# Five groups of instructions kept in the source's order: statistics, square roots, sums on transposes and the inverse's additions

## The chip, the core and the metric

One Trainium2 core runs the whole program. It has five engines, each with a queue of its own that is worked off in order: TensorE for matrix products (PE in the profile; the loads of its stationary operand have a row of their own, PEld), VectorE (DVE), ScalarE (ACT), GpSimd (POOL) and SyncE (SP). DMA transfers are issued from the queues of SP and ACT. The engines meet through semaphores only: an instruction whose operand isn't there yet holds up everything behind it on its own engine. The metric is the device time of one execution in microseconds, as the median of several runs.

## What is computed

`x` holds 32 images of 32 channels of 128 x 128 float32. Two layers with a residual follow each other. The first normalizes pairs of channels and takes a matrix square root of every channel by a Newton-Schulz iteration; the second normalizes again, goes to the frequency domain, mixes channels there for 2 x 32 x 32 modes, and comes back:

```python
    def _L0_conv_ref(A):
        ...
        normA = jnp.sqrt(jnp.sum(A2 * A2, axis=(1, 2)))
        Y = A2 / normA[:, None, None]
        ...
        for _ in range(NUM_ITER):
            T = 0.5 * (3.0 * I - jnp.matmul(Z, Y))
            Y = jnp.matmul(Y, T)
            Z = jnp.matmul(T, Z)
        sA = Y * jnp.sqrt(normA)[:, None, None]
    def _L1_conv_ref(x, weights1, weights2):
        ...
        x_dht = jnp.fft.fftn(x.astype(jnp.complex64), axes=(2, 3)).real
        top = jnp.einsum('bixy,ioxy->boxy', x_dht[:, :, :M1, :M2], weights1)
        bot = jnp.einsum('bixy,ioxy->boxy', x_dht[:, :, -M1:, :M2], weights2)
        ...
        y = jnp.fft.ifftn(out_dht.astype(jnp.complex64), axes=(2, 3)).real
    x = x + _L0_conv_ref(_gn(x))
    x = x + _L1_conv_ref(_gn(x), L1_conv_weights1, L1_conv_weights2)
```

## The kernel before

**The work.** The unit is a group of four channels of one image: 256 groups, eight for each image. A group goes through the generator `newton` in about ten steps. Nine such generators ("lanes") are under way at once; the main loop at the end of the kernel goes round the lanes, and in each round a lane makes one step. Between the lanes the same loop advances the other work: `prep` (first normalization: statistics of two images ahead of their use), `staged` (normalized operands of the next groups), `settle` (what follows when a group is done), `forward` and `spectrum` (towards the frequency domain), the products of the modes, and `inverse` (the way back and the sum that goes to the output). All this is Python that runs when the program is built; the order in which it calls the instructions is what "program order" or "the source's order" means here.

**Who sets the order on an engine.** The instructions go through a scheduler that gives each engine its queue. It may take an instruction earlier than the source has it where, by its own model of time, the operands are there sooner. `kept(...)` (which is `tc.keep_in_program_order`) pins an instruction behind everything that the source has called before on that engine; what comes after it in the source may still be moved ahead of it. So a pinned instruction can only lose the places that the scheduler had let it gain, and those that it had overtaken get them back. Before, the transfers, the operands made in `staged` and the products in `forward` are pinned; most arithmetic isn't.

**What stands around the change.**

- `prep` (L186 on): 16 loads of a tile `xs` for two images, three of them ahead, on the ACT queue (L199), a pool of four buffers; two `bn_stats` on DVE for each (L207) into `a_st`; then the means (L168), two small products on PE (L171, L215), and two calls of `root` (L151), each a Sqrt on ACT (L154) and four or five small DVE instructions, whose results are the scales and offsets `a_sc`, `a_off`, `a_t_s`.
- `staged` (L334 on): four instructions for `x` and four for `b` of a group, on POOL (L349) and ACT (L342), and `plus_eye`, one 128 x 512 addition on POOL into `r` (L295 or L302). A second `plus_eye` for each group stands in `newton`.
- `quartic` (L365 on): for the "far" groups, those of images 1 to 18, a matrix is transposed by way of memory: DVE transposes 32 x 32 blocks into `turn` (L374), SP writes the tile to memory (L376) and reads it back as `w` in another order (L384, L387), POOL adds `r` to it (L389), and one round later PE multiplies by it (through `products`, L308). For all others PE transposes (L314) and DVE adds (L283). Each group has two such places.
- `settle` (L434 on): a finished group's `xt` is stored, and POOL makes `fold` from it in two instructions (L441).
- `summed` (L487 on): the second normalization of an image, with a Sqrt on ACT (L508).
- `inverse` (L841 on): for each half image four PSUM banks `py` are filled (L888). ACT copies two of them into `d` (L900) while DVE adds the other two to `y` (L905), and one round later the roles are swapped. Then POOL adds `d` (L838) and the result is stored. All products share eight PSUM banks.

The far groups end near 1600 us of the profiled execution; `inverse` begins near 1866 us, when the products of the first 20 images are done.

Of the kernel before, what the change touches and what calls it, by code (L numbers as in the profile page):

```python
# [30 lines left out]
AF = mybir.ActivationFunctionType  # L31
ALU = mybir.AluOpType
# [36 lines left out]
def conv_preact_kernel(  # L69
# [81 lines left out]
    def root(v, n, tag):  # L151

        s0 = small.tile([P, n], F32, tag="root_0", name=f"{tag}_s0")
        nc.scalar.activation(s0, v, AF.Sqrt)  # L154
        yield
        q = small.tile([P, n], F32, tag="root_1", name=f"{tag}_q")
        nc.vector.reciprocal(q, s0)
        nc.vector.tensor_mul(q, q, v)
        nc.vector.tensor_tensor(q, q, s0, ALU.add)
        s = small.tile([P, n], F32, tag=f"{tag}_s", name=f"{tag}_s", bufs=2)  # L160
        nc.vector.tensor_scalar_mul(s, q, 0.5)
        return s
# [23 lines left out]
    def prep(bs, made):  # L186

        n = len(bs)
        nc_, ng = n * C, n * G
        first_b = bs[0]  # L190
        st = small.tile([P, ng, 6], F32, tag="a_st", name=f"a_st{first_b}", bufs=2)
        tiles = []
        parts = [(b, i) for b in bs for i in range(C // 4)]

        def load(k):
            b, i = parts[k]
            t = stp.tile([P, 2, 2 * P], F32, tag="xs", name=f"xs{b}_{i}")
            src = xs_in[b, :, 2 * i : 2 * i + 2].rearrange("p g h c -> p g (h c)")
            kept(nc.scalar.dma_start(out=t, in_=src))  # L199
            tiles.append(t)  # L200

        for k in range(3):
            load(k)
        yield
        for k in range(len(parts)):
            for j in range(2):
                nc.vector.bn_stats(st[:, 2 * k + j, :], tiles[k][:, j, :])  # L207
            yield
            if k + 3 < len(parts):
                load(k + 3)  # L210
        ms = small.tile([P, ng], F32, tag="a_ms", name=f"a_ms{first_b}")
        nm, d = yield from moments(st, ms, "a")
        yield from pause
        pq = bank()[:, 0, 0:nc_]
        nc.tensor.matmul(pq, avg_mean, d.rearrange("p g c -> p (g c)"), start=True, stop=True)  # L215

        v = small.tile([P, nc_ + ng], F32, tag="a_v", name=f"a_v{first_b}")
        nc.vector.tensor_scalar_mul(v[:, 0:nc_], pq, -512 / (P * P))
        yield
        vg = small.tile([P, ng], F32, tag="a_vg", name=f"a_vg{first_b}")  # L220
        nc.vector.tensor_reduce(
            vg, v[:, 0:nc_].rearrange("p (g c) -> p g c", c=2), AX.X, ALU.add
        )
        nc.vector.tensor_scalar(v[:, nc_:], vg, 0.5, EPS, ALU.mult, ALU.add)
        yield
        s = yield from root(v, nc_ + ng, "a_r")
        iv = small.tile([P, nc_ + ng], F32, tag="a_inv", name=f"a_inv{first_b}")
        nc.vector.reciprocal(iv, s)
        yield

        sc = small.tile([P, nc_], F32, tag="a_sc", name=f"a_sc{first_b}", bufs=2)
        nc.vector.tensor_scalar_mul(sc, iv[:, 0:nc_], MS / P)
        nn = small.tile([P, ng, 2], F32, tag="a_d", name=f"a_n{first_b}")
        nc.vector.tensor_tensor(  # L234
            nn,
            s[:, 0:nc_].rearrange("p (g c) -> p g c", c=2),
            iv[:, nc_:, None].to_broadcast([P, ng, 2]),
            ALU.mult,
        )
        nn = nn.rearrange("p g c -> p (g c)")  # L240
        nc.vector.tensor_scalar_mul(nn, nn, P * (1.5 / (EYE * QF)) ** 2)
        yield
        sn = yield from root(nn, nc_, "a_t")

        off = small.tile([P, ng, 2], F32, tag="a_off", name=f"a_off{first_b}", bufs=2)
        nc.vector.tensor_tensor(
            off,
            sc.rearrange("p (g c) -> p g c", c=2),
            nm[:, :, None].to_broadcast([P, ng, 2]),
            ALU.mult,  # L250
        )
        off = off.rearrange("p g c -> p (g c)")
        for k, b in enumerate(bs):
            g, c = slice(k * G, k * G + G), slice(k * C, k * C + C)
            made[b] = (nm[:, g], sc[:, c], off[:, c], sn[:, c])
        yield
# [108 lines left out]
    def quartic(m, mb, r, far, more, wide):  # L365


        v = plus(m, -QA * MS, products(mb, m), "v", more)
        if far:


            t = four("turn", more)
            form = "p c (b i) -> p b c i" if wide else "p c (i b) -> p b c i"
            nc.vector.transpose(blocks(t), v.rearrange(form, b=4))  # L374
            held = dram.tile([P, 512], F32, name="turn", tag="turn", bufs=8)
            kept(nc.sync.dma_start(out=held, in_=t.rearrange("p c x -> p (c x)")))  # L376
            yield from rest
            w = four("w", more)
            wb = blocks(w).rearrange("p a c j -> p a (c j)")
            if wide:  # L380
                for b in range(4):
                    rows = slice(32 * b, 32 * b + 32)
                    src = held[:, P * b : P * b + P].rearrange("(a i) x -> i a x", a=4)
                    kept(nc.sync.dma_start(out=wb[rows], in_=src))  # L384
            else:
                src = held.rearrange("(a i) (b x) -> (i b) a x", a=4, b=4)
                kept(nc.sync.dma_start(out=wb, in_=src))  # L387
            yield from rest
            nc.gpsimd.tensor_tensor(w, w, r, ALU.add)  # L389
            w = blocks(w).rearrange("p a c j -> p c a j")  # L390
        else:
            yield from rest
            w = plus(transposed(v), 1.0, r, "w", more)
        yield from rest
        q = plus(products(v, w), QF / (16 * MS**4), eye, "q", more)
        yield from rest
        return q
# [89 lines left out]
    def summed(b, st):  # L487

        mq = small.tile([P, 2, G], F32, tag="b_mq", name=f"b_mq{b}")
        _, d = yield from moments(st, mq[:, 0, :], "b")  # L490
        yield

        nc.vector.tensor_reduce(mq[:, 1, :], d, AX.X, ALU.add)
        wide = small.tile([P, 2, G, 2], F32, tag="b_wide", name=f"b_wide{b}")
        nc.vector.tensor_copy(wide, mq[:, :, :, None].to_broadcast([P, 2, G, 2]))
        wide = wide.rearrange("p k g c -> p k (g c)")
        yield from pause
        pv = bank()[:, 0, :]
        for i in range(4):
            rows = slice(C * i, C * i + C)  # L500
            nc.tensor.matmul(pv[rows, 0:1], wide[:, 1, :], avg_v, start=True, stop=True)
        nc.tensor.matmul(pv[0:C, 1:2], wide[:, 0, :], avg_0, start=True, stop=True)
        v = small.tile([P, 2], F32, tag="b_v", name=f"b_v{b}")
        nc.vector.tensor_scalar(v[:, 0:1], pv[:, 0:1], 1.0, EPS, ALU.mult, ALU.add)
        nc.vector.tensor_copy(v[0:C, 1:2], pv[0:C, 1:2])
        yield
        s = small.tile([P, 3], F32, tag="b_r", name=f"b_r{b}")
        nc.scalar.activation(s[:, 0:1], v[:, 0:1], AF.Sqrt)  # L508
        yield
        nc.vector.reciprocal(s[:, 1:2], s[:, 0:1])  # L510
        nc.vector.tensor_scalar(
            s[:, 2:3], v[:, 0:1], s[:, 1:2], s[:, 1:2], ALU.mult, ALU.mult
        )
        nc.vector.tensor_scalar(s[:, 2:3], s[:, 2:3], -0.5, 1.5, ALU.mult, ALU.add)
        r = small.tile([P, 1], F32, tag="b_inv", name=f"b_inv{b}")
        nc.vector.tensor_mul(r, s[:, 1:2], s[:, 2:3])
        scales[b] = v, r
        yield
# [322 lines left out]
    def inverse(b):  # L841
# [37 lines left out]
        for e in range(2):  # L879
# [16 lines left out]
            for i in range(2):  # L896

                for j in range(2):
                    n = 2 * (1 - i) + j
                    nc.scalar.copy(d[:, 4 * n : 4 * n + 4, :], py[n][:, :, 64:128])  # L900
                for j in range(2):
                    y = yts[b, e][i][:, 4 * j : 4 * j + 4, :]
                    y = y.rearrange("p c (s h) -> p c s h", s=2)
                    half = py[2 * i + j][:, :, None, 0:64].to_broadcast([P, 4, 2, 64])
                    nc.vector.tensor_tensor(y, half, y, ALU.add)  # L905
                unfold()
                sums.append((b, 16 * e + 8 * i, yts[b, e][i], d[:, 8 * i : 8 * i + 8, :]))
                if not i:
                    holding.append(b)
                    yield  # L910
                    holding.pop()
# [201 lines left out]
```

## Time and profile before

| | |
|---|---|
| median of 3 runs | 3047.77 us (3047.1 to 3060.3) |
| profiled execution: its own time / span | 3058.61 us / 3056.7 us |
| mean granted TensorE clock | 0.978 |
| busy: PE / DVE / POOL / ACT | 2901.3 / 2238.3 / 1999.1 / 1638.1 us |
| 512 `bn_stats` on DVE (L207) | 195.8 us, 412 ns each |
| 288 additions on `w` on POOL (L389) | 366.6 us, 1276 ns each |
| 34 + 32 Sqrt on ACT (L154, L508) | about 0.24 us each |
| DMA, mean | 208 GB/s |

The table is read from top to bottom: PE has the most work, and the other engines have a fifth to a half of the span free. A time that an engine waits costs the kernel something only if PE, which follows its own fixed queue, then finds an operand missing or a PSUM bank still in use.

### The profile page before, as it was taken

Reading aid. Unit: us, or ns where it says so; the run is one execution under the profiler, and the core shown is the slowest. Engines: PE = TensorE matmul, PEld = TensorE weight load, DVE = VectorE, ACT = ScalarE, POOL = GpSimd, SP = SyncE. Lnnn points to the kernel's source line nnn. Section 1 sums busy time; section 2 is a strip of 40 time slices with the busy share of each in tenths; the row PEclk is TensorE's granted clock in tenths of the full one; section 3 lists DMA queues with packets and bytes.
Section 4 is the critical chain, followed back from the end, with each engine's and each line's share of the span. In section 5 each row is a group of like instructions: output and inputs, shape, how many; then the busy total and the mean of one; then the engine's idle time right before and its main releaser. Section 6 shows DMA issues by size and latency. Waiting matters only on the chain.

```text
span 3056.7 us, 73392 instructions
## 1 busy us (share of the span) xinstructions
PE 2901.3 (95%) x27076; PEld 2697.1 (88%) x27076; DVE 2238.3 (73%) x4255; ACT 1638.1 (54%) x4187; POOL 1999.1 (65%) x2312
## 2 busy tenths in 40 slices
PE   6999999999999999999999999999899998999994
PEld 6899999999999999999999888898898887888883
DVE  6778787878787878777866545777777765867664
ACT  3566566566565566565545544454454444555552
POOL 4577777776767777777755435676676763777452
PEclk9999999999999999999999999999999998999996
DMA  5476766767576768676733666677667667665675
GB/s 168 159 229 209 218 210 219 222 204 226 187 231 194 242 193 247 186 245 189 232 101 115 190 199 223 204 247 241 205 216 247 219 232 231 205 205 199 194 242 202
DMA packets 476659, 636.40 MB, mean 208 GB/s; under 512 B 97040, under 2 KB 257296, under 8 KB 476304
## 3 DMA queue, kind: packets, MB, share of 16 engines
q1 hardware_dynamic: 362976, 424.31, 43.3%
q10 hardware_dynamic: 113328, 207.41, 21.7%
q8 instruction: 217, 3.56, 0.5%
q14 instruction: 138, 1.13, 0.1%
HBM read 402.42 MB, written 229.11 MB: 207 GB/s over the span
## 4 chain that ended last, share of the span: by engine, by line
PE 76%; DMA 11%; DVE 5%; POOL 3%; ACT 2%; issue 2%; SPq 1%; ACTq 0%; DVEq 0%; POOLq 0%
PE ps L308 50%; PE ps L418 12%; PE ps L314 6%; DMA xs<-in_xs 4%; PE ps L464 2%; DMA w<-turn 1%; PE ps L888 1%; DMA or<-od 1%; PE ps L617 1%; POOL yt L838 1%; PE ps L870 1%; PE ps L529 1%; DVE yt L905 1%; DMA plain<-in_wk 1%; DVE a_st L207 1%
## 5 line engine op out<-in xcount | busy, mean ns | idle before, releaser
L308 PE MATMUL ps<-w,v 128*128 128x128 f32 x4096 | 555.8, 279 | 16.3 <-POOL w L389 6.6
L389 POOL TENSOR_TENSOR w<-w,r 128x512 f32<-128x512 f32 x288 | 366.6, 1276 | 306.5 <-DMA w<-turn 249.5
L342 ACT ACTIVATE b<-b,a_off,a_sc 128x128 f32<-128x128 f32 x1024 | 467.3, 490 | 160.4 <-issue 48.0
L308 PEld LDWEIGHTS ps<-w,v 128*128 128x128 f32 x4096 | 507.6, 194 | 29.2 <-POOL w L389 8.3
L418 PE MATMUL ps<-my,q 128*128 128x256 f32 x2048 | 491.6, 383 | 9.6 <-ACT d L900 6.0
L441 POOL TENSOR_TENSOR fold<-xt 128x256 f32<-128x256 f32 x512 | 364.6, 734 | 170.2 <-DVE xt L428 155.9
L283 DVE SCALAR_TENSOR_TENSOR q<-ps,eye 128x512 f32<-128x512 f32 x512 | 348.2, 680 | 164.4 <-PE ps L308 158.3
L838 POOL TENSOR_TENSOR yt<-yt,d 128x512 f32<-128x512 f32 x248 | 310.5, 1282 | 197.2 <-ACT d L900 150.6
L418 PEld LDWEIGHTS ps<-my,q 128*128 128x128 f32 x2048 | 370.5, 191 | 56.6 <-ACT d L900 6.8
L349 POOL TENSOR_SCALAR x<-xt,a_nm,a_sc 128x128 f32<-128x128 f32 x736 | 324.1, 455 | 18.6 <-DVE a_n L234 18.6
L302 POOL TENSOR_TENSOR r<-mb,eye 128x512 f32<-128x512 f32 x112 | 142.8, 1275 | 295.5 <-ACT mb L275 282.3
L421 ACT ACTIVATE t<-ps 128x256 f32<-128x256 f32 x512 | 192.8, 383 | 231.4 <-PE ps L418 226.5
L424 ACT ACTIVATE y<-ps,a_t_s 128x128 f32<-128x128 f32 x1024 | 312.0, 370 | 0.0
L207 DVE BATCH_NORM_STATS2 a_st<-xs 128x6 f32<-128x256 f32 x512 | 195.8, 412 | 139.1 <-DMA xs<-in_xs 138.6
L308 PE MATMUL ps<-y,t 128*128 128x128 f32 x2048 | 276.5, 279 | 10.4 <-DVE t L283 9.6
L308 PE MATMUL ps<-x,q 128*128 128x128 f32 x2048 | 278.2, 279 | 6.2 <-DVE q L283 6.2
L308 PE MATMUL ps<-x,b 128*128 128x128 f32 x2048 | 277.9, 279 | 5.9 <-POOL x L349 5.7
L407 ACT ACTIVATE my<-ps 128x512 f32<-128x512 f32 x256 | 152.9, 597 | 243.0 <-PE ps L308 238.0
L308 PE MATMUL ps<-my,mb 128*128 128x128 f32 x2048 | 277.3, 279 | 3.1 <-ACT d L900 3.1
L308 PE MATMUL ps<-my,q 128*128 128x128 f32 x2048 | 277.7, 279 | 2.1 <-ACT my L407 2.1
L308 PE MATMUL ps<-q,t 128*128 128x128 f32 x2048 | 275.2, 278 | 1.2 <-ACT d L900 1.2
L308 PEld LDWEIGHTS ps<-my,q 128*128 128x128 f32 x2048 | 262.4, 194 | 14.6 <-issue 2.7
(138 smaller groups left out, 5572.4 us busy)
## 6 DMA issues: line engine op xcount, KB each, us to landing
turn<-turn SPq DMA_DIRECT2D x288, 256.0 KB
b<-in_x ACTq DMA_DIRECT2D x256, 256.0 KB
xt<-in_xt ACTq DMA_DIRECT2D x256, 256.0 KB
xs<-in_xs ACTq DMA_DIRECT2D x256, 256.0 KB
mid<-xt SPq DMA_DIRECT2D x256, 256.0 KB
yt<-mid SPq DMA_DIRECT2D x128, 512.0 KB
out<-yt SPq DMA_DIRECT2D x117, 512.0 KB
w<-turn SPq DMA_DIRECT2D x144, 256.0 KB
```

Source lines behind the costliest of these rows:

```text
L207: nc.vector.bn_stats(st[:, 2 * k + j, :], tiles[k][:, j, :])
L283: nc.vector.scalar_tensor_tensor(s, ps, f, t, ALU.mult, ALU.add)
L308: nc.tensor.matmul(ps[:, j, :], lhsT[:, j], rhs[:, j], start=True, stop=True)
L314: nc.tensor.transpose(ps[:, j, :], t[:, j, :], ident)
L342: nc.scalar.activation(t, x, AF.Identity, bias=offset[:, c], scale=scale[:, c])
L349: nc.gpsimd.tensor_scalar(m[:, j, :], xt[:, j, :], nm[:, c // 2 : c // 2 + 1], sc[:, c : c + 1], ALU.add, ALU.mult,)
L389: nc.gpsimd.tensor_tensor(w, w, r, ALU.add)
L418: nc.tensor.matmul(both[j // 2][:, j % 2], q[:, j], my[:, j], start=True, stop=True)
L421: nc.scalar.mul(w[:, 2 * h : 2 * h + 2, :], both[h][:, :, 1, :], 1 / (MS * QF))
L424: nc.scalar.mul(y[:, j, :], both[j // 2][:, j % 2, 0, :], sn[:, c : c + 1])
L441: nc.gpsimd.tensor_tensor(f[:, :, 64 * half : 64 * half + 64], xt[:, :, 0:64], xt[:, :, 64:128], op)
L838: engine.tensor_tensor(yh, yh, d, op)
```

## The change

`kept` is put around five calls, and nothing else is touched. No instruction is added or removed, and no operand changes.

```diff
     def root(v, n, tag):
...
-        nc.scalar.activation(s0, v, AF.Sqrt)
+        kept(nc.scalar.activation(s0, v, AF.Sqrt))
...
             for j in range(2):
-                nc.vector.bn_stats(st[:, 2 * k + j, :], tiles[k][:, j, :])
+                kept(nc.vector.bn_stats(st[:, 2 * k + j, :], tiles[k][:, j, :]))
...
             yield from rest
-            nc.gpsimd.tensor_tensor(w, w, r, ALU.add)
+            kept(nc.gpsimd.tensor_tensor(w, w, r, ALU.add))
             w = blocks(w).rearrange("p a c j -> p c a j")
...
         s = small.tile([P, 3], F32, tag="b_r", name=f"b_r{b}")
-        nc.scalar.activation(s[:, 0:1], v[:, 0:1], AF.Sqrt)
+        kept(nc.scalar.activation(s[:, 0:1], v[:, 0:1], AF.Sqrt))
...
                     half = py[2 * i + j][:, :, None, 0:64].to_broadcast([P, 4, 2, 64])
-                    nc.vector.tensor_tensor(y, half, y, ALU.add)
+                    kept(nc.vector.tensor_tensor(y, half, y, ALU.add))
```

When both kernels are built and their queues are compared place by place, PE and SP have exactly the same order in both. On the other three engines:

| engine | pinned | what the pin moves | what moves ahead in its stead |
|---|---|---|---|
| DVE | `bn_stats` L207 | 394 of 512 later, up to 20 places | 566 of 1248 of L283 (`v`, `w`, `q`, `t`), 98 of 256 `xt` (L428), 95 of 288 `turn` (L374), up to 14 places |
| DVE | `yt` L905 | 63 of 256 later, up to 7 places | 86 of 256 stand earlier, up to 13 places, since statistics and root arithmetic left their way |
| ACT | Sqrt L154, L508 | 29 of 34 and 5 of 32 later, up to 29 places | copies of the Newton steps, by at most 5 places |
| POOL | `w` L389 | 139 of 288 later, up to 6 places | 141 of 288 `r` (L295), 126 of 736 `x` (L349), 78 of 512 `fold` (L441), by at most 2 places |

All 139 additions on `w` that move lie in the first 1600 us of the profile of before.

## The prediction

> **What bounds the kernel now.** I read the page's first two parts, then PE by stretches.
>
> ```profile
> span 3056.7 us, 73392 instructions
> PE 2901.3 (95%) x27076; PEld 2697.1 (88%) x27076; DVE 2238.3 (73%) x4255; ACT 1638.1 (54%) x4187; POOL 1999.1 (65%) x2312
> ...
> 76.00:1600.00 1524.00, 1513.06 (x12627) 1434.54 (x12626) 1215.33 (x2313) 905.20 (x2349) 1085.09 (x1209) 1.00 0.67 208
> 1866.00:2980.00 1114.00, 1047.20 (x10751) 952.94 (x10751) 788.57 (x1447) 559.12 (x1422) 738.70 (x866) 0.97 0.68 221
> ```
>
> The stretches' columns are bounds, length, busy time of PE, PEld, DVE, ACT, POOL, then granted clock, DMA share, GB/s. PE is the bound, but in two ways. From 76 to 1600 us it is idle for 10.9 us of 1524, at clock 1.00: nothing to win there, much to lose. From 1866 to 2980 it is idle for 66.8 us and the clock averages 0.97: something can be won there. PE's own queue doesn't change, so the question is only which operand or bank is late for it.
>
> The waits name the places:
>
> ```profile
> ACT d L900 <- DVE yt L905: 160.4, 61, 6.3
> DVE a_st L207 <- DMA xs<-in_xs: 138.6, 83, 6.5
> POOL w L389 <- DMA w<-turn: 249.5, 114, 5.8
> ```
>
> DVE waits 138.6 us for statistics whose data haven't landed: they were put too early. ACT waits 160.4 us for `yt`. The timeline shows both in one event of the late stretch:
>
> ```profile
> 2131.62 0.43 DVE L207 BATCH_NORM_STATS2 a_st<-xs 128x6 f32<-128x256 f32 x1 [4.07 <-DMA xs<-in_xs]
> 2131.97 1.27 DVE L905 TENSOR_TENSOR yt<-ps,yt 128x512 f32<-128x512 f32 x2
> 2132.67 0.92 ACT L900 COPY d<-ps 128x256 f32<-128x256 f32 x3 [6.24 <-DVE yt L905]
> 2133.10 1.67 PE L308 MATMUL ps<-w,v 128*128 128x128 f32 x8 [2.42 <-ACT d L900]
> ```
>
> One `bn_stats` waits 4.07 us for its load; `yt` is queued behind it; ACT's copy of the same bank waits 6.24 us for `yt`; PE waits 2.42 us for the bank.
>
> **The change, part by part.**
>
> *Statistics, roots and `yt` on DVE and ACT: a gain, late.* In the changed queue that `bn_stats` stands 20 places later, behind the `yt` pair; the runs of four statistics or of root arithmetic ahead of other `yt` pairs are gone as well. From PE's waits of 1866 to 2980 I add those released by ACT `d` (6.9 + 6.0 + 0.4), DVE `q` (4.7 + 1.8), `w` 2.8, `t` (2.7 + 1.0), `v` 1.7, `a_t_q` 0.9, ACT `my` 4.2 and `z` 3.9: 37 us. Left out are 29 us of other waits (weights and products from memory, `ob`, `b_wide`, `fold`, `gt`), which the change doesn't reach.
>
> Such a wait has a second price. After the one shown, PE's granted clock is 0.57 from 2133.1 to 2136.5; it comes back after 3.4 us, in which half the work is done, so some 1.7 us more. Going through the timeline, ten such slow intervals (eight of some 3.4 us with two of 6.8, 41 us together) follow the waits that I counted; at half speed that is 20 us. A full gain would be 57 us. Against it: 63 of the 256 `yt` additions go later by up to 7 places, 0.68 us each (L283's row); these are mostly a half image's second pair, which now stands a round later and keeps two of the eight PSUM banks in the meantime. If a quarter of the 63 met a PE waiting for the bank, by one place each, 11 us would go back, and other waits of that size remain. I take 40 us; bounds 10 and 57.
>
> *Cover for what is pinned later.* The roots' results have time: `a_off` is written at 906.9 and first read at 950.1 us, the others 34 to 90 us ahead, against at most 25 places on DVE or 29 on ACT, under 20 us. The means `a_ms` move by at most 12 places, 9 us, and PE takes them 18 us or more after their end where they move most, 5.5 us or more elsewhere, where they move by at most 7 (3.8 us). Cost nothing; without that cover PE would wait at L171, 17 times, a few us each. Later statistics also free their `xs` buffer later, and the load that wants it stands in ACT's queue, with all copies of the Newton steps behind it. The load comes two steps of `prep` after the statistics of its buffer, 7 us or more; nothing again, and 12.1 us is what ACT loses to this release now (its wait on `a_st` at L342).
>
> *The sum on POOL: a loss, early.* `w` is different: PE takes it one round after it is called, and it is now queued behind `r`, `x` and `fold` of other groups. `fold` waits for `xt`, which DVE has only just been asked for. An instance:
>
> ```profile
> 1173.46 1.28 POOL L295 TENSOR_TENSOR r<-mb,eye 128x512 f32<-128x512 f32 x1
> 1174.69 1.30 POOL L389 TENSOR_TENSOR w<-w,r 128x512 f32<-128x512 f32 x1
> 1175.84 0.64 DVE L428 TENSOR_TENSOR xt<-ps,xt 128x512 f32<-128x512 f32 x1
> 1178.19 1.45 POOL L441 TENSOR_TENSOR fold<-xt 128x256 f32<-128x256 f32 x2
> 1178.26 1.06 PE L308 MATMUL ps<-w,v 128*128 128x128 f32 x8
> 1179.61 0.89 POOL L349 TENSOR_SCALAR x<-xt,a_nm,a_sc 128x128 f32<-128x128 f32 x2
> 1180.45 1.28 POOL L295 TENSOR_TENSOR r<-b,eye 128x512 f32<-128x512 f32 x1
> ```
>
> The `w` of 1174.69 ends at 1175.99; PE multiplies by it at 1178.26, a margin of 2.3 us. In the changed queue two `fold`, two `x` and one `r` come first. `fold` can't start before `xt` ends at 1176.5 (DVE's order gives `xt` no earlier place here): 1176.5 + 1.45 + 0.89 + 1.28 + 1.30 = 1181.4, so PE waits 3.2 us.
>
> I did this sum for all 139 that move: start of each instruction now ahead no sooner than its operand in this trace, `w` no sooner than its transfer landed, 1.276 us for it, and `xt` put earlier where statistics leave its way on DVE. 107 are still in time (the median margin of a moved `w` was 4.2 us). 32 come late, by 57 us together; 70 us if `xt` gains nothing. 11 of them exceed 2.1 us; every wait of PE over that in this trace is followed by a slow interval, most by 3.4 us. The 4.2 us wait at 139.9, which has this very pattern already (`r`, two `x`, `w`), is followed by clock 0.53 from 144.0 to 150.8 with PE busy for 4.86 of 6.8 us, so a slow 3.4 us costs 1.7 x 4.86 / 6.8 = 1.2 us: 11 x 1.2 = 13. I take 57 + 13 = 70 us. Upper bound: 70 plus 20 waits of 1.6 us or more at the full 1.7, 34: 104. Lower bound from what stands in this order already: of 11 `w` that directly follow two `fold`, two `x` and one `r` in this trace, two kept PE waiting (4.2 and 1.9 us); 48 of the moved get a `fold` ahead, 48 x 2 / 11 x 3.0 us = 26.
>
> [...]
>
> `r`, `x`, `v`, `q` and `turn` that come earlier in this stretch win at most PE's 10.9 us of idle time, of which `w` itself causes 6.6; I take nothing.
>
> *Start and end.* The first 46 us of DVE's queue are the same as before, and of PE's last 77 us the waits hang on one image's chain: nothing.
>
> **Sum.** 70 - 40 = +30 us on 3058.6 us, 1.0%. The profiled execution lies 10.8 us above the median of the runs; set on the median: 3047.8 + 30 = 3078. Under 0.5%, 15 us, I call it no change, about what the spread of the three runs (13 us) lets one tell.
>
> **Rivals.**
>
> *The sums keep their margin, and the late gain stays.* POOL is 71% busy in the early stretch, so it could catch up, and a PE that waited once gives the next `w` its wait as margin. For it: 9 of 11 in the same order are in time. Against it: the moved ones are those that a late `fold` separates from their place, and most of the late ones lie 20 to 60 us apart, too far to share a wait. Price: 26 + 5 of clock - 57 = -26: 3022.
>
> *The two cancel.* Loss near 55, gain near 50: within 15 us of 3048.
>
> *The second `yt` pair takes the banks.* This ends well above: the half image's banks 3 and 4 are held a round longer, PE waits for them at the next allocation, and the late gain shrinks to 10. It decides once the release falls behind the eighth following use of a bank, 7 to 8 us of PE work at 0.9 us a bank. For it: PE's largest waits there are for just these banks. Against it: most such pairs move by one or two places only. 3048 + 70 - 10 = 3108.
>
> That the change doesn't do what it says is excluded by the queues as built.
>
> **Numbers.** Forecast (3063 to 3100) 0.45; sums keep their margin 0.27; cancel 0.13; banks 0.15. Slower 0.45 + 0.15 = 0.60, same 0.13, faster 0.27. Range: all at its worst is 3048 + 104 - 10 = 3142 and at its best 3048 + 26 - 57 = 3017; the worst needs every bound at once, so I cut it to 3120, and give the best 5 us for waits of ACT that I counted as nothing: 3012.
>
> **What would show it.** Right: PE's wait on POOL `w` L389 grows from 6.6 to 40 us or more before 1600, with a granted clock below 1.00 there and POOL `fold` directly ahead of late `w`; DVE's wait on `xs` falls from 138.6 to under 30, ACT's on `yt` from 160.4 to about half, PE's on ACT `d` from 13 to under 4; 1866 to 2980's stretch is shorter by some 40 us. Wrong: the stretch to 1600 us keeps its length (then the first rival), or new waits of PE on `yt` L905 appear (the last one).

## The result and the profile after

The changed kernel takes 3072.32 us (median of 7 runs, 3064.6 to 3082.47), the kernel before in the same sitting 3048.67 us (7 runs, 3047.1 to 3060.3). The ratio is 1.0082, with an interval of 1.0061 to 1.0103: slower by 24 us. The profiled execution took 3078.48 us, 6 us above the median of its kernel; that of before lay 10 us above its own.

The first two parts of the changed kernel's page, and PE by stretches (columns as before). PE's queue is the same in both kernels, so the bounds are set where the same PE instructions stand; 77.30 to 1672.69 answers to 76 to 1600 of before, and 1937.25 to 2999.34 to 1866 to 2980:

```profile
span 3076.5 us, 73387 instructions
PE 2900.9 (94%) x27076; PEld 2696.2 (88%) x27076; DVE 2244.6 (73%) x4255; ACT 1640.8 (53%) x4187; POOL 1996.1 (65%) x2312
...
77.30:1672.69 1595.39, 1533.29 (x12628) 1448.83 (x12626) 1219.20 (x2316) 908.44 (x2349) 1083.43 (x1209) 0.99 0.64 198
1672.69:1937.25 264.56, 261.30 (x2913) 239.82 (x2912) 152.75 (x303) 128.80 (x310) 123.61 (x170) 1.00 0.56 172
1937.25:2999.34 1062.09, 1022.86 (x10751) 933.92 (x10750) 789.26 (x1445) 558.55 (x1423) 736.44 (x865) 0.99 0.71 232
```

The same work takes 71.4 us longer early on (1595.4 against 1524.0) and 51.9 us less late (1062.1 against 1114.0); the piece between the two stretches, the start and the end make up +0.3. That is the whole difference of the spans, 19.8 us. Length minus PE's busy time is its idle time: early it goes from 10.9 to 62.1 us, late from 66.8 to 39.2. The rest is busy time of the same PE instructions: 20.2 us more early (granted clock 1.00 to 0.99) and 24.3 us less late (0.97 to 0.99).

The waits of the whole run (who waits, on whom: sum in us, how many, the longest):

```profile
ACT d L900 <- DVE yt L905: 137.2, 59, 7.1
POOL w L389 <- DMA w<-turn: 78.6, 49, 3.8
PE ps L308 <- POOL w L389: 59.8, 31, 3.2
DVE a_st L207 <- DMA xs<-in_xs: 25.3, 16, 6.4
```

DVE hardly waits for `xs` any more (138.6 before), and POOL waits less for transposes from memory (249.5), since its `w` now comes later. But PE waits for that `w` 31 times, 59.8 us; before it was three times, 6.6 us.

The loss can be read in the very place for which the prediction worked out a wait of 3.2 us, in the changed kernel's timeline (start, duration, engine, line and operation; in brackets the idle time before it and who ended it):

```profile
1231.38 1.44 POOL L441 TENSOR_TENSOR fold<-xt 128x256 f32<-128x256 f32 x2 [1.81 <-DVE xt L428]
1232.81 0.87 POOL L349 TENSOR_SCALAR x<-xt,a_nm,a_sc 128x128 f32<-128x128 f32 x2
1233.65 1.25 POOL L295 TENSOR_TENSOR r<-b,eye 128x512 f32<-128x512 f32 x1
1234.87 2.48 POOL L389 TENSOR_TENSOR w<-w,r 128x512 f32<-128x512 f32 x2
1236.18 1.87 PE L308 MATMUL ps<-w,v 128*128 128x128 f32 x8 [3.19 <-POOL w L389]
```

`fold` waits 1.81 us for `xt`, then `fold`, `x` and `r` run, and only then `w`: PE stands for 3.19 us. In two stretches of 3.4 us of the same trace, before and after that moment, the clock is the third number from the end:

```profile
1233.00:1236.40 3.40, 0.22 (x2) 0.22 (x3) 1.67 (x4) 1.14 (x3) 3.40 (x5) 1.00 0.89 311
1236.00:1239.40 3.40, 3.22 (x16) 3.22 (x17) 1.31 (x4) 0.72 (x2) 2.58 (x3) 0.56 0.86 274
```

PE works through the 3.4 us after its wait at a granted clock of 0.56. The gain can be read where before one `bn_stats` waited 4.07 us for its load (at 2131.62 there); the same event in the changed kernel:

```profile
2176.96 1.15 PE L888 MATMUL ps<-gt,tab 32*128 32x260 f32 x16
2177.51 0.67 DVE L283 SCALAR_TENSOR_TENSOR q<-ps,eye 128x512 f32<-128x512 f32 x1
2178.12 1.29 DVE L905 TENSOR_TENSOR yt<-ps,yt 128x512 f32<-128x512 f32 x2
2178.85 0.92 ACT L900 COPY d<-ps 128x256 f32<-128x256 f32 x3 [2.21 <-DVE yt L905]
2180.72 1.06 PE L308 MATMUL ps<-w,v 128*128 128x128 f32 x8
```

No statistics stand ahead of `yt`; ACT's copy waits 2.21 us instead of 6.24, and PE (last line) finds its bank free and doesn't wait, where it waited 2.42.

### The profile page after: what moved, and what is told of

Its sections match the earlier page's. It is cut to its first block, busy times and chain, and to the rows that moved or that the text cites. A ratio compares the mean times of both kernels' runs of the same rounds, so it can differ in the third digit from the quotient of the medians.

```text
span 3076.5 us, 73387 instructions
## 1 busy us (share of the span) xinstructions
PE 2900.9 (94%) x27076; PEld 2696.2 (88%) x27076; DVE 2244.6 (73%) x4255; ACT 1640.8 (53%) x4187; POOL 1996.1 (65%) x2312
## 4 chain that ended last, share of the span: by engine, by line
PE 57%; DMA 6%; DVE 5%; POOL 4%; issue 2%; ACT 1%; SPq 1%; ACTq 0%; POOLq 0%; DVEq 0%
PE ps L308 36%; PE ps L418 9%; PE ps L314 5%; PE ps L888 2%; PE ps L464 1%; PE ps L617 1%; PE ps L870 1%; DVE yt L905 1%; POOL w L389 1%; DMA w<-turn 1%; POOL r L295 1%; POOL fold L441 1%; PE ps L529 1%; PE ps L687 1%; DMA yt<-mid 1%
## 5 line engine op out<-in xcount | busy, mean ns | idle before, releaser
L308 PE MATMUL ps<-w,v 128*128 128x128 f32 x4096 | 557.6, 280 | 68.7 <-POOL w L389 59.8
L308 PEld LDWEIGHTS ps<-w,v 128*128 128x128 f32 x4096 | 506.6, 194 | 85.8 <-POOL w L389 67.3
L441 POOL TENSOR_TENSOR fold<-xt 128x256 f32<-128x256 f32 x512 | 364.0, 732 | 253.6 <-DVE xt L428 196.5
L283 DVE SCALAR_TENSOR_TENSOR q<-ps,eye 128x512 f32<-128x512 f32 x512 | 349.7, 683 | 234.4 <-PE ps L308 229.1
L389 POOL TENSOR_TENSOR w<-w,r 128x512 f32<-128x512 f32 x288 | 365.6, 1274 | 97.0 <-DMA w<-turn 78.6
L349 POOL TENSOR_SCALAR x<-xt,a_nm,a_sc 128x128 f32<-128x128 f32 x736 | 322.5, 450 | 18.5 <-DVE a_n L234 18.5
L295 POOL TENSOR_TENSOR r<-b,eye 128x512 f32<-128x512 f32 x144 | 183.8, 1276 | 171.7 <-ACT b L342 123.8
L308 PE MATMUL ps<-x,b 128*128 128x128 f32 x2048 | 286.0, 285 | 5.9 <-POOL x L349 5.7
L308 PE MATMUL ps<-y,t 128*128 128x128 f32 x2048 | 275.8, 278 | 9.2 <-DVE t L283 8.0
L308 PE MATMUL ps<-x,q 128*128 128x128 f32 x2048 | 275.9, 278 | 3.0 <-DVE q L283 2.4
L308 PE MATMUL ps<-my,q 128*128 128x128 f32 x2048 | 275.8, 278 | 2.1 <-ACT my L407 2.1
L308 PE MATMUL ps<-q,t 128*128 128x128 f32 x2048 | 275.4, 278 | 0.0
L308 PE MATMUL ps<-my,mb 128*128 128x128 f32 x2048 | 273.4, 277 | 0.0
L308 PEld LDWEIGHTS ps<-my,q 128*128 128x128 f32 x2048 | 260.4, 193 | 14.5 <-issue 2.7
```

Source lines behind the costliest of these rows:

```text
L283: nc.vector.scalar_tensor_tensor(s, ps, f, t, ALU.mult, ALU.add)
L295: nc.gpsimd.tensor_tensor(blocks(r).rearrange("p a c j -> p c a j"), mb.rearrange("p c (a j) -> p c a j", a=4), eye.rearrange("p c (a j) - ...
L308: nc.tensor.matmul(ps[:, j, :], lhsT[:, j], rhs[:, j], start=True, stop=True)
L349: nc.gpsimd.tensor_scalar(m[:, j, :], xt[:, j, :], nm[:, c // 2 : c // 2 + 1], sc[:, c : c + 1], ALU.add, ALU.mult,)
L389: kept(nc.gpsimd.tensor_tensor(w, w, r, ALU.add))
L441: nc.gpsimd.tensor_tensor(f[:, :, 64 * half : 64 * half + 64], xt[:, :, 0:64], xt[:, :, 64:128], op)
```

## The experiments

Before each group the kernel before was timed on the same chip: 3047.55 us beside the first four, 3049.97 beside the next four, 3048.49 beside the last two. "Wait on `w`" is PE's wait at L308 on POOL's addition, "wait on `xs`" is DVE's at L207 on its loads.

| | time, us | ratio to before, with interval | wait on `w` | wait on `xs` |
|---|---|---|---|---|
| the change | 3072.32 | 1.0082 [1.0061, 1.0103] | 59.8 | 25.3 |
| e1 `w` alone | 3125.27 | 1.0244 [1.0216, 1.0271] | 62.2 | 134.9 |
| e2 all but `w` | 3007.36 | 0.9863 [0.9838, 0.9888] | 8.1 | 28.7 |
| e3 statistics alone | 3008.06 | 0.9869 [0.9844, 0.9894] | 8.3 | 30.8 |
| e4 `yt` alone | 3042.36 | 0.9991 [0.9970, 1.0013] | 8.5 | 151.8 |
| e5 Sqrt alone | 3056.76 | 1.0028 [1.0011, 1.0045] | 8.9 | 157.2 |
| e6 `w`, with `fold` later | 3106.91 | 1.0179 [1.0164, 1.0194] | 59.2 | 145.9 |
| e8 `w`, with `r` later | 3072.76 | 1.0062 [1.0037, 1.0087] | 23.4 | 154.9 |
| e9 `w`, with both later | 3069.05 | 1.0064 [1.0045, 1.0082] | 20.1 | 149.2 |
| e7 statistics, loads two ahead | 3021.32 | 0.9905 [0.9881, 0.9929] | 6.4 | 97.3 |
| e11 the change, with `r` later | 3013.99 | 0.9883 [0.9854, 0.9912] | 16.2 | 26.6 |

**e1 and e2: the sum alone, and everything but the sum.** The theory: a loss early, by `w` alone, and a gain late, by the rest. The rival: they work on the same waits, and neither shows its size by itself. e1 has this pin and no other; e2 has the other four:

```diff
             yield from rest
-            nc.gpsimd.tensor_tensor(w, w, r, ALU.add)
+            kept(nc.gpsimd.tensor_tensor(w, w, r, ALU.add))
```

> Only the addition on w (L389) is pinned. Theory: this pin is the whole loss of the change, and lies before 1680 us: PE waits for POOL w about 60 us in some 30 places there (57 in my sum; 59.8 in the changed kernel), clock adds some 13, so 55 to 80 us over before, 3105 to 3130; the late stretch keeps its waits on ACT d and DVE. Rival (the loss belongs to the five pins together, w is late because DVE's new order makes xt late): PE waits for w under 30 us and the time is below 3080.

> All pins but that on w. Theory: the gain of the late stretch alone, 40 to 57 us under before: 2992 to 3010, with PE waiting for w under 7 us as before. Rival (the gain in the late stretch is only time made up after the earlier delay, PE having been late there): within 15 us of before, 3034 to 3064.

Both came out as the theory had it: +78 us and -40 us between the medians. PE by stretches in e1, bounds at the same PE instructions again:

```profile
76.19:1671.93 1595.74, 1531.49 (x12627) 1447.49 (x12626) 1221.41 (x2313) 906.96 (x2349) 1082.76 (x1209) 0.99 0.64 198
1938.49:3037.44 1098.95, 1037.26 (x10751) 942.63 (x10750) 786.92 (x1447) 559.52 (x1423) 738.20 (x866) 0.98 0.69 224
```

The early stretch is as long as with the whole change (1595.7 against 1595.4): the loss is the sum's. The late one lies 15 us under that of before without any reason in its queues, which shows how far the late stretch can lie apart in single executions. So does this: the span of e1's profiled execution is 56 us above that of before, where the medians differ by 78.

**e3, e4 and e5: the gain taken apart.** The same line of one kind each is pinned:

```diff
-                nc.vector.bn_stats(st[:, 2 * k + j, :], tiles[k][:, j, :])
+                kept(nc.vector.bn_stats(st[:, 2 * k + j, :], tiles[k][:, j, :]))
```

```diff
-                    nc.vector.tensor_tensor(y, half, y, ALU.add)
+                    kept(nc.vector.tensor_tensor(y, half, y, ALU.add))
```

```diff
-        nc.scalar.activation(s0, v, AF.Sqrt)
+        kept(nc.scalar.activation(s0, v, AF.Sqrt))
...
-        nc.scalar.activation(s[:, 0:1], v[:, 0:1], AF.Sqrt)
+        kept(nc.scalar.activation(s[:, 0:1], v[:, 0:1], AF.Sqrt))
```

> Only bn_stats (L207) is pinned. Theory: the statistics that wait for their load ahead of yt are most of the late gain, 25 to 45 us under before: 3004 to 3024, DVE's wait on xs falls from 138.6 to under 40 us. Rival (it is the place of yt that counts): under 10 us gain, 3039 or more.

> Only the inverse's additions (L905) are pinned. Theory: a pin never moves an instruction earlier, so the first pairs still stand behind the statistics; the second pairs stand later and keep banks: no change or up to 15 us more, 3044 to 3064, ACT's wait on yt stays near 160 us. Rival (the place of yt is what brings the gain): 15 us or more under before, below 3034.

> Only the square roots (L154, L508) are pinned. Theory: their results have 34 to 90 us to spare and the arithmetic that they hold back is a small part of what stands ahead of yt, so under 10 us gain: 3038 to 3055, DVE's wait for xs stays above 120 us. Rival (a third of the late gain comes from the root arithmetic leaving yt's way): 3034 or less.

PE by stretches with the statistics alone:

```profile
76.21:1601.72 1525.51, 1512.92 (x12627) 1434.00 (x12626) 1218.26 (x2316) 906.04 (x2349) 1084.33 (x1209) 1.00 0.67 207
1868.25:2928.84 1060.59, 1020.32 (x10751) 931.32 (x10750) 789.03 (x1447) 559.39 (x1423) 738.06 (x866) 0.99 0.71 232
```

The early stretch is that of before (1525.5 against 1524.0), the late one that of the changed kernel (1060.6 against 1062.1). So the statistics carry the whole gain; `yt` and the two Sqrt added to them (e2) change nothing more. `yt` alone makes no difference that its interval tells from none; its median lies 2 us under the expected range. The two Sqrt alone cost 0.1 to 0.45%, some 8 us, and end 2 us above the expected range. Where is not settled: in the profiled execution of e5 the early stretch takes 1532.8 us against 1524.0 before, with PE idle for 17.3 us in place of 10.9, and the late one 1105.7 against 1114.0; in e2, which has these pins too, the early stretch takes 1527.3.

**e6: which neighbour makes `w` late, `fold`?** The prediction named `fold`. Here e1 has its two additions called one round later, so that `xt` is there by then; the queues of PE, DVE, ACT and SP are those of e1:

```diff
     def settle(b, g, st, xt):
...
-        if g % 2 == 0:
-            folds[b, g // 2] = sets.tile([P, 8, P], F32, tag="fold", name=f"fold{b}_{g}", bufs=3)
-        f = folds[b, g // 2][:, 4 * (g % 2) : 4 * (g % 2) + 4, :]
-        for half, op in enumerate((ALU.add, ALU.subtract)):
-            nc.gpsimd.tensor_tensor(
...
         yield
+        if g % 2 == 0:
...
+            nc.gpsimd.tensor_tensor(
```

> The sum on w pinned as in e1 (3125 us, PE waits 62 us for POOL w), and the two fold instructions of a group called one step (a round) later in settle; the queues of PE, DVE, ACT and SP stay as in e1. Theory: w is late because it stands behind instructions whose own operand has just been asked for, fold (needs xt) and r (needs ACT's b). Done without fold, my sum over the trace of before gives 17 us of late w in place of 70: PE's wait for w falls to 15 to 30 us, time 3065 to 3090. Rival (it is the POOL work as such that stands ahead, 0.73 to 1.28 us apiece; a fold moved from one w stands ahead of another): wait stays above 45 us, time above 3105.

That theory missed. The time, though by the ratios some 20 us under e1's, stays above the point that the rival had named, and the wait on `w` is 59.2 us against e1's 62.2. The `fold` taken away from one `w` stands ahead of the next, as in this place of its timeline:

```profile
1419.86 1.26 POOL L389 TENSOR_TENSOR w<-w,r 128x512 f32<-128x512 f32 x1 [5.72 <-DMA turn<-turn]
1421.08 1.40 POOL L448 TENSOR_TENSOR fold<-xt 128x256 f32<-128x256 f32 x2
1422.44 1.26 POOL L295 TENSOR_TENSOR r<-b,eye 128x512 f32<-128x512 f32 x1
1423.66 1.26 POOL L389 TENSOR_TENSOR w<-w,r 128x512 f32<-128x512 f32 x1
...
1424.97 1.44 PE L308 MATMUL ps<-w,v 128*128 128x128 f32 x5 [5.89 <-POOL w L389]
```

One pinned `w` waits 5.72 us for its own transfer; `fold` and `r` follow; then comes the `w` for which PE waits 5.89 us. So a pinned `w` is also held up by another pinned `w`, not only by `fold`. Nor was `fold` out of the way: for 15 of the 27 late `w` of e6, 27.8 of the 59.2 us, POOL's last idle time ahead of `w` still stands before a `fold`; for nine, 26.6 us, before a `w`.

**e8 and e9: `r` a round later, and both.** The waits of POOL in the early stretch, first before, then with the change, had another candidate:

```profile
POOL w L389 <- DMA w<-turn: 249.5, 114, 5.8
POOL fold L441 <- DVE xt L428: 63.7, 49, 6.1
POOL r L295 <- ACT b L342: 23.0, 16, 3.6
POOL r L295 <- ACT mb L275: 15.0, 10, 6.0
```

```profile
POOL r L295 <- ACT b L342: 123.8, 40, 6.0
POOL fold L441 <- DVE xt L428: 108.6, 48, 6.9
POOL w L389 <- DMA w<-turn: 78.6, 49, 3.8
POOL r L295 <- ACT mb L275: 58.4, 31, 5.5
```

`fold`'s wait for `xt` grew by 45 us, but that of `r` for the operand `b`, which ACT makes in the step just before it, by 101 us. `staged` calls `r` one step after the last `b`; before, `w` was let past `r`. e8 is e1 with `r` called a round (nine steps) later, e9 has this and the edit of e6:

```diff
             on_scalar(mb[:, j, :], mb[:, j, :], off, sc, c)
             yield
+        for _ in range(LANES):
+            yield
         ready.append((xt, m, mb, plus_eye(mb, is_far(b), has_more(b, g))))
```

> The sum on w pinned as in e1, and in staged the addition r (L295, L302 after staging) called nine lane steps (one round) later. Theory: without these r ahead, the same sum gives 28 us: PE's wait for w 20 to 40 us, time 3075 to 3100. Rival (POOL work as such): wait stays above 45 us, time above 3105.

> The sum on w pinned, fold and r both a round later. Theory: nothing that waits is left ahead of w; PE's wait for w under 12 us, time within 15 us of before, 3034 to 3064. Rival (the pin itself, or POOL's load, costs): above 3080.

The waits that the edit aims at, in e8 (lines below it are shifted by two):

```profile
POOL r L295 <- ACT b L342: 41.4, 24, 3.8
PE ps L308 <- POOL w L391: 23.4, 16, 6.1
```

The wait of `r` falls from 123.1 us in e1 to 41.4, PE's on `w` from 62.2 to 23.4, and the time by 52 us, a little more than expected: of the neighbours tried, `r` is the main one. All of that lies in the early stretch, which takes 1544.0 us in e8 and 1595.7 in e1.

What `r` costs is mostly its own work, though, and not its wait for `b`. In e1 an `r` on `b` runs ahead of 29 of the 32 late `w`, behind POOL's last idle time; an estimate from that trace, each late `w` without the 1.27 us of this one `r`, leaves 27.2 of the 62.2 us, and e8 measured 23.4. Only for three of the 32, 4.7 us, does that last idle time stand before an `r`. e9 missed: with `fold` later as well, 20.1 us of waits on `w` stay, and the time is the same as e8's. Its largest wait on `w` shows what remains:

```profile
1049.59 1.43 POOL L450 TENSOR_TENSOR fold<-xt 128x256 f32<-128x256 f32 x2 [5.22 <-DVE xt L430]
1050.97 1.28 POOL L295 TENSOR_TENSOR r<-mb,eye 128x512 f32<-128x512 f32 x1
1052.19 1.28 POOL L295 TENSOR_TENSOR r<-b,eye 128x512 f32<-128x512 f32 x1
1053.41 2.50 POOL L391 TENSOR_TENSOR w<-w,r 128x512 f32<-128x512 f32 x2
...
1054.74 1.65 PE L308 MATMUL ps<-w,v 128*128 128x128 f32 x6 [5.41 <-POOL w L391]
```

Even a round later `fold` waits 5.22 us for `xt` here, and two `r` go ahead of `w`.

**e7: does the gain hang on the loads?** In e3 the loads are three ahead of the statistics. Here they are two ahead:

```diff
-        for k in range(3):
+        for k in range(2):
             load(k)
...
-            if k + 3 < len(parts):
-                load(k + 3)
+            if k + 2 < len(parts):
+                load(k + 2)
```

> bn_stats pinned as in e3 (3008 us, DVE waits 31 us for xs), but the loads of xs run two tiles ahead instead of three. Theory: what the pin takes away is DVE's wait for a load that hasn't landed, so with the data a step of prep later the wait comes back: DVE waits 60 us or more for xs, and 10 us or more of the 40 us gain are lost, 3018 or more. Rival (the gain is the place alone: yt no longer behind four statistics of 0.33 us each, whatever the loads do): below 3013.

As expected: the wait on `xs` comes back to 97.3 us, and by the ratios 11 of e3's 40 us are lost. But most of the 97.3 us lie early, where they cost PE little: the early stretch takes 1527.7 us against e3's 1525.5. What counts is DVE's wait in the late stretch, before and in e7 (in e3 it is 2.3 us):

```profile
DVE a_st L207 <- DMA xs<-in_xs: 69.3, 30, 5.7
```

```profile
DVE a_st L207 <- DMA xs<-in_xs: 25.0, 13, 5.4
```

About a third of that wait comes back, and a quarter of the gain goes: the late stretch takes 1072.3 us against 1060.6. So part of what the pin brings is that a load has landed when its statistics' turn comes. How much of the rest is that alone, and how much that `yt` has no statistics ahead of it at all, this run doesn't separate.

**e11: the changed kernel with `r` a round later.** The edit of e8 on the whole change.

> The changed kernel with r called a round later in staged, as in e8. Theory: the loss of the change hangs on r ahead of w as in e1, so some 45 to 55 us come back, as from e1 to e8 (52): 3017 to 3030, PE's wait for w 15 to 30 us, below before. Rival (with DVE in its new order other instructions hold up w): PE's wait for w stays above 40 us and the time above 3055.

Slightly better than expected: 3013.99 us against the change's 3072.32. PE's wait on `w` is 16.2 us. This confirms within the changed kernel itself that `w` behind `r` is most of the loss. It doesn't beat e2 and e3, which leave the sum unpinned: both are 1.3% faster than the kernel before and faster than the changed kernel.

## Why the prediction was right, and where not

It said +30 us, 3078, from a loss of 70 early and a gain of 40 late; measured were +24 between the medians, and by stretches of the profiles 71.4 and 51.9.

- **The loss.** Late `w` were put at 32, 57 us together; the trace has 31, 59.8 us in all, where before three waits took 6.6. The chosen instance came out at 3.19 us for 3.2. The clock was put at 13 us; PE's busy time grew by 20.2, some 15 of which the slow intervals account for (last section). In the 6.8 us from 144.0 of before, PE was busy for 6.69 us; the 4.86 that the price of a slow interval was worked out from are those of L308 alone. That 57 comes so close to 59.8 doesn't vouch for the sum, and may in part be luck: the same sum gave 17 us without `fold`, where e6 has 59.2, and 28 without `r`, where e8 has 23.4.
- **Its reason.** The text named `fold`'s wait for `xt`, and the trace of the changed kernel bears it out. Followed back on POOL from each late `w`, POOL's last idle time stands before a `fold` for 23 of the 31, 47.3 of the 59.8 us, 20 of them waiting for `xt`; for five, 7.2 us, before `w` itself or an earlier `w`; for three, 5.2 us, before `r`. From there POOL works through to `w` without a gap, and 29 times `r` is the last instruction ahead of it. The sum counted `r`'s time; what the text missed is what removing either would do. A `fold` called later takes its wait to another `w` (e6); without the `r` ahead of it a late `w` comes up to 1.27 us earlier, and the 31 are late by 1.9 us on average (e8).
- **The gain.** The mechanism was right, and e3 shows that it is the statistics'. PE's idle time late fell by 27.6 of the 37 us counted, its busy time by 24.3, against 20 estimated for the clock. Nothing of the 11 us that were to be given back by later `yt` showed up; on the profiles the term of 40 is 12 short, which the execution profiled of before largely explains: six others without pinned statistics (e1, e4, e5, e6, e8, e9) took 1092 to 1106 us for that stretch, and before's took 1114. Between the medians the gain is 40 (e2, e3).
- **One sign was read wrongly.** ACT's wait on `yt` was to fall to about half; it fell from 160.4 to 137.2 us. PE's wait on ACT `d` in the late stretch went from 13.3 to 0.6 all the same. ACT may wait long for `yt` as long as its copy still ends before PE wants the bank. Before, seven copies ended too late; five of them stood behind statistics that waited for `xs`. The other two, 2.45 and 0.17 us, stood behind the roots' arithmetic, and e3, which doesn't pin the roots, still has these two at 2.44 and 0.17.
- **That every wait over 2.1 us is followed by a slow interval failed.** It holds in the trace of before from 76 to 2980 us, for all 16 of them. In the changed kernel's early stretch 13 waits on `w` exceed 2.1 us; eight are followed by a clock of 0.50, five are not. The last section has what went with it.
- **The rivals.** The sums didn't keep their margin, and loss and gain didn't cancel. The second `yt` pair didn't take the banks: in the changed kernel's trace PE never waits for `yt` L905, and e4 is no slower than before. Sqrt at nothing is not settled (e5).

Open: the 20 us that stay ahead of `w` in e9 were seen in some places, not accounted for in full; the 8 us of e5; what `r` called later does to a kernel whose `w` isn't pinned, which no run has; and why the parts don't add up: +78 (e1) and -40 (e2) would make +38, the change has +24. The spans of the profiled executions miss the other way, +56 and -45 against +20, so it may be no more than the spread of single executions.

## What to carry to other kernels

Pin an instruction to its place in the source if the scheduler's model lets it pass too early, as with statistics whose load hasn't landed: that was worth 40 us here. Don't pin one that the source calls right behind instructions whose operands have only just been asked for: on a queue worked off in order it inherits their waits and their work, and that cost 78 us. So a bundle of pins is to be taken apart; the losing one hid a version that beats both.

## What the runs showed of the hardware

No wait of PE on `w` in the changed kernel exceeds 3.2 us, and still the granted clock fell to 0.50 after some of them, for 3.4 us or twice that. The length of the wait alone didn't decide it: of two waits of 2.90 us the one at 287.3 was followed by it and the one at 1043.8 was not, and two of 1.95 and 1.98 us were. Slow intervals took 41 us of that stretch, against 10 us before; at a clock of 0.50 the added 31 us account, by estimate, for some 15 of the 20 us by which PE's busy time grew.

What went with it can be read from the two traces, that of before and that of the changed kernel. In each, all changes of the granted clock lie whole multiples of 3.413 us apart, to within 0.005 us, so the trace can be cut at these moments into equal cells, and PE's idle time in a cell can be set beside the clock of the next. Between 76 and 2980 us of the two traces the clock fell 36 times (19 before, 17 with the change), each time at the end of a cell with at least 1.6 us of idle time. After a cell at full clock with 2.0 us or more it fell every time; between 1.6 and 2.0 us either happened (a fall after 1.62 us, none after 1.91). The two waits of 2.90 us, with the clock again third from the end:

```profile
287.53:290.94 3.41, 0.72 (x6) 0.72 (x7) 2.68 (x4) 1.33 (x3) 3.41 (x4) 1.00 0.65 197
290.94:294.35 3.41, 3.41 (x15) 3.23 (x15) 1.87 (x5) 0.00 (x0) 1.68 (x2) 0.50 1.04 256
1041.87:1045.28 3.41, 1.90 (x18) 1.66 (x16) 2.98 (x6) 1.18 (x2) 3.39 (x5) 1.00 0.70 236
1045.28:1048.70 3.42, 2.03 (x17) 2.03 (x18) 0.83 (x2) 0.88 (x2) 3.42 (x4) 1.00 1.03 260
1048.70:1052.11 3.41, 3.41 (x26) 3.20 (x25) 2.88 (x6) 2.00 (x7) 0.37 (x1) 1.00 0.87 267
```

The first wait lies almost whole in one cell, where PE is busy for only 0.72 us; the second is cut in two by the end of a cell, 1.5 and 1.4 us, and the clock stays at 1.00. Of the 13 waits on `w` over 2.1 us, the eight that were followed by half the clock leave 1.97 us or more of idle time in one cell, the five others at most 1.78.
